# A Mamba scan layer driven by a plan of stages instead of a generator of parts

## The chip, the cores and the metric

The kernel runs on one core of a Trainium2 chip. Its time is device microseconds of one execution, the median of several. The engines that matter here: TensorE (PE, matmuls into PSUM), VectorE (DVE), ScalarE (ACT), GpSimd (POOL), and SyncE (SP), whose queue issues all DMAs of the scan layer.

## The reference, cut to what matters

Four layers run one after the other on x of 3 images, 256 channels, 48 x 48 pixels: an attention block, two 3x3 convolutions, and a Mamba layer. Only the last one is touched by the change. Its input gets a scale and a shift per channel (from the normalisation around each layer), and then, for each image with its 2304 pixels as a sequence of length L:

```python
xn = (xf - mu) * jax.lax.rsqrt(var + 1e-05) * norm_w + norm_b
xz = jnp.einsum('blc,dc->bld', xn, in_proj_w)
x_in, z = jnp.split(xz, 2, axis=-1)
xc = jax.lax.conv_general_dilated(xc, conv_w, ...)   # causal, 4 taps, per channel
u = jax.nn.silu(xc).transpose(0, 2, 1)
x_dbl = jnp.einsum('bld,ed->ble', u, x_proj_w)       # dt_raw (16), B (16), C (16)
dt = jax.nn.softplus(jnp.einsum('blr,dr->bld', dt_raw, dt_proj_w) + dt_proj_b)
def step(hst, inp):
    dA = jnp.exp(dt_t[:, :, None] * A)
    hst = hst * dA + dt_t[:, :, None] * B_t[:, None, :] * u_t[:, :, None]
    y_t = jnp.einsum('bdn,bn->bd', hst, C_t)
y = ys.transpose(1, 0, 2) + u * D_param
y = y * jax.nn.silu(z)
out = jnp.einsum('bld,cd->blc', y, out_proj_w)
```

There are 512 inner channels d with 16 states n each, and the result is added to x.

## The kernel before

All of it is float32. The sequence of each image is cut into 6 chunks of 384 tokens (CH), which makes 18 chunks over the 3 images. A chunk has 16 **steps** j = 4m + g: m is one of 4 blocks of 128 inner channels, g one of 4 groups of states. A step scans 4 x 128 rows of 384 tokens, a row being one channel and one state. The layer has 288 steps.

One step s consists of these instructions:

- `fill(s + 1)` prepares the input dt*B*u of the next step in a tile hs: DVE does one half (L939, reading PSUM tile ps_r, which PE's `spread_pe` L921 has filled), POOL the other (L940).
- DVE runs four scans (L1045), which are called q0 to q3 here. Each needs one decay exp(dt*A), which ACT writes to one of three PSUM banks (`decay`, L952). The decay three scans ahead is issued after each scan.
- ACT keeps the last column of the four scans for the next chunk (L1053). POOL multiplies hs by C into hc (L1056).
- PE adds the four parts of hc of the step before to y in PSUM (`add_states(s - 1)`, L968; at g = 0 a product with D opens the sum, L964).
- In steps with g = 1, DVE multiplies the finished y of the block before by sz, the Silu of z (`gate`, L975), and SP fetches dt and dt*u of the next block, copied over the partitions (`spread`, L912 and L913). The copies come from DRAM, where dt has been written.

Beside the scans of one chunk runs the **preparation** of the next, the generator `prepare`: scale and shift (ACT L770), mean by matmul (PE L778), centring (DVE L780, square on ACT L784), mean of squares (PE L787), inverse root (ACT L789, L790), normalise (DVE L792), tokens (ACT L802), the convolution as four taps times two channel halves of matmuls per block m (PE L823, 16 recorded matmuls per block), taking u to SBUF (ACT L815, L829), z (PE L844, ACT L849), Silu of u and of z back to back (ACT L853, L854), the projection of u (PE L860), B and C through DRAM (ACT L865), dt by matmul in two halves (PE L883), softplus in three ACT passes (L889 to L891), and dt and dt*u (DVE L894, L895, ACT L898). All PSUM results of it use one buffer of two banks, of which `two()` hands out a new tile for each use. Silu lies in another table set of ACT than Exp and Ln, so that a table load stands ahead of the two Silus and another (`exp_ln_tables`, L748) after them. The program calls the generator twice per step, at its very start, ahead of fill and scans, and after hc; each call runs to the next `yield`. Preparation of chunk at + 2 begins in steps 12 to 15 of chunk at.

What is finished of a chunk is projected in steps 2 and 3 of the next one (`project`, PE L988) and both halves stored at step 4, ahead of the fill (`store`, DVE L996); the residual's load is issued at step 1.

Ahead of the first step the whole preparation of chunk 0 and eight parts of chunk 1's (to the tokens) are run through.

`keep_order` ties the instructions of PE, DVE, ACT and POOL to the order in which the program writes them. An instruction whose input isn't there holds up all that is written after it on its engine. The DMAs of SP aren't tied by it.

Of the kernel before, what the change touches and what calls it, by code (L numbers as in the profile page):

```python
# [16 lines left out]
P = 128  # L17
# [60 lines left out]
def net(  # L78
# [618 lines left out]
    with ExitStack() as l3:  # L697
# [52 lines left out]
        def fetch(at):  # L750
            k = chunks[at] = Chunk()
            b, c = todo[at]
            k.xg = act.tile([P, CT, CH], F32, name="xg")
            nc.sync.dma_start(k.xg, xd[b][:, :, c * CH : (c + 1) * CH])
# [4 lines left out]
        def two():  # L759
            return psg.tile([P, 2, 512], F32, tag="g", name="ps_g")  # L760

        def prepare(at, before, k):


            b, c = todo[at]
            sc, sh = norm3[b]
            xg = k.xg

            for ct in range(CT):
                nc.scalar.activation(  # L770
                    xg[:, ct, :], xg[:, ct, :], AF.Identity,
                    bias=sh[:, ct : ct + 1], scale=sc[:, ct : ct + 1],
                )
            yield
            p = two()
            pm, pv = p[:, 0, :CH], p[:, 1, :CH]
            for ct in range(CT):
                nc.tensor.matmul(pm, mean2, xg[:, ct, :], start=ct == 0, stop=ct == CT - 1)  # L778
            yield
            nc.vector.tensor_tensor(  # L780
                xg, xg, pm.unsqueeze(1).broadcast_to([P, CT, CH]), ALU.subtract
            )
            sq = act.tile([P, CT, CH], F32, name="sq", bufs=1)
            nc.scalar.activation(sq, xg, AF.Square)  # L784
            yield
            for ct in range(CT):
                nc.tensor.matmul(pv, mean2, sq[:, ct, :], start=ct == 0, stop=ct == CT - 1)  # L787
            yield
            nc.scalar.activation(pv, pv, AF.Ln, bias=epst)  # L789
            nc.scalar.activation(pv, pv, AF.Exp, scale=-0.5)  # L790
            yield
            nc.vector.tensor_tensor(  # L792
                xg, xg, pv.unsqueeze(1).broadcast_to([P, CT, CH]), ALU.mult
            )
            yield
            xn = k.xn = act.tile([P, CT, CH + DCONV - 1], F32, name="xn")
            if c == 0:
                nc.gpsimd.memset(xn[:, :, : DCONV - 1], 0.0)
            else:
                nc.scalar.copy(xn[:, :, : DCONV - 1], before.xn[:, :, CH:])  # L800
            for ct in range(CT):
                nc.scalar.activation(  # L802
                    xn[:, ct, DCONV - 1 :], xg[:, ct, :], AF.Identity,
                    bias=v("norm_b", ct), scale=v("norm_w", ct),
                )
            yield
            yield
            u = k.u = act.tile([P, DI, CH], F32, name="u")
            for m0 in (0, 2):

                p = None
                for j in range(2):
                    m = m0 + j
                    if j:
                        nc.scalar.activation(  # L815
                            u[:, m0, :], p[:, 0, :CH], AF.Identity, bias=v("conv_b", m0)
                        )
                    yield
                    if not j:
                        p = two()  # L820
                    for tap in range(DCONV):
                        for ct in range(CT):
                            nc.tensor.matmul(  # L823
                                p[:, j, :CH], wtap[:, tap, ct, m * P : (m + 1) * P],
                                xn[:, ct, tap : tap + CH],
                                start=tap == 0 and ct == 0, stop=tap == DCONV - 1 and ct == CT - 1,
                            )
                    yield
                nc.scalar.activation(  # L829
                    u[:, m0 + 1, :], p[:, 1, :CH], AF.Identity, bias=v("conv_b", m0 + 1)  # L830
                )
                if m0 == 0:

                    for _ in range(4):
                        yield

            yield
            sz = k.sz = act.tile([P, DI, CH], F32, name="sz")
            for m0 in (0, 2):
                p = two()  # L840
                for j in range(2):
                    m = m0 + j
                    for ct in range(CT):
                        nc.tensor.matmul(  # L844
                            p[:, j, :CH], w("in", ct * 512 + m * P, P), xn[:, ct, DCONV - 1 :],
                            start=ct == 0, stop=ct == CT - 1,
                        )
                yield
                nc.scalar.copy(sz[:, m0 : m0 + 2, :], p[:, :, :CH])  # L849
                if m0 == 0:  # L850
                    yield

            nc.scalar.activation(u, u, AF.Silu)  # L853
            nc.scalar.activation(sz, sz, AF.Silu)  # L854
            exp_ln_tables()
            yield

            p = two()
            for m in range(DI):
                nc.tensor.matmul(  # L860
                    p[:96, 0, :CH], w("x", m * 96, 96), u[:, m, :], start=m == 0, stop=m == DI - 1
                )
            yield
            dbc = act.tile([96, CH], F32, name="dbc")
            nc.scalar.activation(dbc, p[:96, 0, :CH], AF.Identity, bias=ident[:96, DTR : DTR + 1])  # L865
# [9 lines left out]
            yield  # L875

            dt = act.tile([P, DI, CH], F32, name="dt", bufs=1)
            dtu = k.dtu = act.tile([P, DI, CH], F32, name="dtu")
            for m0 in (0, 2):
                p = two()  # L880
                for j in range(2):
                    m = m0 + j
                    nc.tensor.matmul(  # L883
                        p[:, j, :CH], dtsb[:, m * P : (m + 1) * P], dbc[: DTR + 1, :],
                        start=True, stop=True,
                    )
                yield
                both = dt[:, m0 : m0 + 2, :]
                nc.scalar.activation(both, p[:, :, :CH], AF.Abs)  # L889
                nc.scalar.activation(both, both, AF.Exp, scale=-1.0)  # L890
                nc.scalar.activation(both, both, AF.Ln, bias=1.0)  # L891
                yield
                pdt = p[:, :, :CH]
                nc.vector.scalar_tensor_tensor(pdt, pdt, 0.0, both, ALU.max, ALU.add)  # L894
                nc.vector.tensor_tensor(  # L895
                    dtu[:, m0 : m0 + 2, :], pdt, u[:, m0 : m0 + 2, :], ALU.mult
                )
                nc.scalar.copy(both, pdt)  # L898

            k.dtd = dram.tile([P, DI, CH], F32, name="dtd")  # L900
            nc.sync.dma_start(k.dtd, dt)
            k.dtud = dram.tile([P // 2, DI, CH], F32, name="dtud")
            nc.sync.dma_start(k.dtud, dtu[P // 2 :])
            yield
# [72 lines left out]
        def residual(at):  # L977
            k = chunks[at]
            b, c = todo[at]
            k.ot = act.tile([P, CT, CH], F32, name="ot")  # L980
            nc.sync.dma_start(k.ot, xd[b][:, :, c * CH : (c + 1) * CH])

        def project(at, mo):
            k = chunks[at]
            if mo == 0:
                k.po = two()
            for m in range(DI):
                nc.tensor.matmul(  # L988
                    k.po[:, mo, :CH], w("out", m * 256 + mo * P, P), k.sz[:, m, :],
                    start=m == 0, stop=m == DI - 1,  # L990
                )

        def store(at, mo):
            k = chunks[at]
            b, c = todo[at]
            nc.vector.tensor_tensor(k.ot[:, mo, :], k.po[:, mo, :CH], k.ot[:, mo, :], ALU.add)  # L996
            nc.sync.dma_start(
                out[b, mo * P : (mo + 1) * P, c * CH : (c + 1) * CH], k.ot[:, mo, :]
            )

# [7 lines left out]
        for _ in prepare(0, None, chunks[0]):  # L1008
            pass
        k = chunks[0]  # L1010
        k.rows = {0: spread(k, 0)}
# [4 lines left out]
        parts = {1: prepare(1, k, chunks[1])}  # L1016
        for _ in range(8):
            next(parts[1])

        def part(at):  # L1020
            if at in parts:
                next(parts[at], None)

        for s, (at, m, g) in enumerate(steps):
            k = chunks[at]
            j = 4 * m + g


            if j == 0 and at + 2 <= last:
                fetch(at + 2)  # L1030
            if j == 12 and at + 2 <= last:
                parts[at + 2] = prepare(at + 2, chunks[at + 1], chunks[at + 2])
            mine = at + 2 if j >= 12 else at + 1
            part(mine)
# [151 lines left out]
```

## Time and profile before

| | |
|---|---|
| median of 3 runs | 4667.45 us (4663.21 to 4670.96) |
| the profiled execution | 4670.4 us, span 4668.6 us |
| first fill of the loop over steps | 3001.76 us |
| start of chunk 1 and of chunk 17 | 3093.58 and 4566.38 us |
| end of the last chunk | 4647.95 us |
| DVE scans with a state (L1045) | x960, 998 ns each by the page |
| decays (L952) | x1152, 581 ns |
| hc (L1056) | x288, 3442 ns |
| POOL's half of fill (L940) | x288, 1815 ns |
| DVE's half of fill (L939) | x288, 944 ns |

The page's shares of busy time are averages over four layers: the first 3000 us belong to the attention and the convolutions, in which PE leads. For the scan layer the profile must be read from 3000 us on. Mean durations overlap a little where instructions of one engine follow each other without a gap: a scan takes 1.0 us in the rows, but the next one starts 0.91 us after it. PE's matmuls run at one of two paces: with the granted clock at 1.0 those of 384 columns are some 0.35 us apart, with the clock at 0.5 some 0.64.

### The profile page before, as it was taken

The page shows a single profiled execution, that of the slowest core. Times are in us where ns is not written, and L with a number is a line of the kernel's source. Part 1 is how long each engine was busy: PE and PEld are TensorE (multiplying, and loading weights), DVE is VectorE, ACT ScalarE, POOL GpSimd, SP SyncE. Part 2 cuts the span into 40 slices and gives each one's busy share as a digit, 9 for nine tenths or more (in the row PEclk, how much of TensorE's full clock was granted, in tenths as well). Part 3 has the DMA queues.
Part 4 walks back from the last instruction along what each step waited for, and adds up shares of the span by engine and source line. Part 5 has one row for each costly group of instructions (what it writes and reads, how often), then busy time and mean ns, then how long its engine had stood idle before and what let it go on. Part 6 is the DMA issues. An engine that isn't in the chain of part 4 may idle for free. (4 is left out here: it accounts for less than half of the span.)

```text
span 4668.6 us, 47523 instructions
## 1 busy us (share of the span) xinstructions
PE 3832.0 (82%) x18498; PEld 1603.0 (34%) x18498; DVE 2840.0 (61%) x2936; ACT 2205.5 (47%) x3196; POOL 1547.2 (33%) x662
## 2 busy tenths in 40 slices
PE   7999999789999976269999998677787777778774
PEld 4322222332322222135555554332333233223321
DVE  4677767357686732640001111388888888888887
ACT  1577767137776755200000000366656666665663
POOL 0000000000000001000000000288998899899888
PEclk9999999899999976589999998787888788788875
DMA  2000000000000001310000001233334333343332
GB/s 79 3 1 1 1 1 1 0 1 1 1 1 1 1 28 31 124 61 0 0 0 0 21 20 58 62 92 100 87 94 101 96 90 100 89 104 91 88 94 51
DMA packets 122319, 207.65 MB, mean 44 GB/s; under 512 B 20881, under 2 KB 114129, under 8 KB 118370
## 3 DMA queue, kind: packets, MB, share of 16 engines
q1 hardware_dynamic: 122082, 204.50, 16.2%
q8 instruction: 147, 2.41, 0.2%
q14 instruction: 90, 0.74, 0.1%
HBM read 167.94 MB, written 36.27 MB: 44 GB/s over the span
## 5 line engine op out<-in xcount | busy, mean ns | idle before, releaser
L387 ACT ACTIVATE pt<-ps_s 128x1024 f32<-128x1024 f32 (+1 forms) x1080 | 952.4, 937 | 363.7 <-PE ps_s L383 306.9
L1056 POOL TENSOR_TENSOR hc<-hs,bc 128x1536 f32<-128x1536 f32 x288 | 991.3, 3442 | 170.3 <-DVE hs L1045 154.5
L1045 DVE TENSOR_TENSOR_SCAN hs<-ps_da,hst,hs 128x384 f32<-128x384 f32 x960 | 902.6, 998 | 134.1 <-ACT ps_da L952 131.2
L952 ACT ACTIVATE ps_da<-dtr,amat 128x384 f32<-128x384 f32 x1152 | 653.5, 581 | 363.4 <-DVE hs L1045 345.3
L394 DVE TENSOR_TENSOR part<-part,pt 128x2048 f32<-128x2048 f32 (+1 forms) x360 | 747.8, 2077 | 40.7 <-ACT pt L387 9.4
L147 POOL TENSOR_TENSOR rstd<-ve,mhalf 128x2 f32<-128x2 f32 (+1 forms) x26 | 16.1, 623 | 1957.5 <-DVE ve L145 1957.5
L383 PE MATMUL ps_s<-q,kt 32*128 32x512 f32 (+1 forms) x4320 | 645.2, 603 | 13.0 <-ACT pt L387 7.0
L940 POOL TENSOR_TENSOR hs<-dtur,bc 128x768 f32<-128x768 f32 x288 | 522.6, 1815 | 90.8 <-DMA dtr<-dtd 90.8
L362 PE MATMUL acc<-pt,vt 128*32 128x512 f32 (+1 forms) x4320 | 535.5, 565 | 0.0
L637 PE MATMUL ps_c<-xpad,wmix 128*128 128x384 f32 x1296 | 421.0, 487 | 100.4 <-DVE wmix L678 100.4
L637 PE MATMUL ps_c<-xpad,wconv 128*128 128x384 f32 x1296 | 423.9, 490 | 8.9 <-DVE xpad L623 8.9
L823 PE MATMUL ps_g<-xn,wtap 128*128 128x384 f32 x1152 | 416.1, 516 | 15.1 <-DVE ot L996 5.3
L619 ACT ACTIVATE xpad<-x,gsh,gsc 128x2304 f32<-128x2304 f32 x6 | 13.9, 2320 | 820.7 <-DVE gsh L178 578.2
L968 PE MATMUL ps_y<-hc,rep 128*32 128x384 f32 x2304 | 302.6, 611 | 117.1 <-POOL hc L1056 106.6
L383 PEld LDWEIGHTS ps_s<-q,kt 32*128 32x128 f32 x4320 | 216.4, 184 | 449.4 <-issue 256.2
L637 PEld LDWEIGHTS ps_c<-xpad,wmix 128*128 128x128 f32 x1296 | 246.0, 190 | 274.8 <-DVE wmix L678 100.5
L637 PEld LDWEIGHTS ps_c<-xpad,wconv 128*128 128x128 f32 x1296 | 247.2, 191 | 184.0 <-issue 13.7
L823 PEld LDWEIGHTS ps_g<-xn,wtap 128*128 128x128 f32 x1152 | 224.9, 201 | 219.6 <-issue 26.0
L939 DVE TENSOR_TENSOR hs<-ps_r,bc 128x768 f32<-128x768 f32 x288 | 272.0, 944 | 4.6 <-PE ps_r L921 4.6
L647 DVE TENSOR_TENSOR x<-ps_c,x 128x384 f32<-128x384 f32 x36 | 20.1, 558 | 382.5 <-PE ps_c L637 382.5
L649 DVE SCALAR_TENSOR_TENSOR x<-ps_c,vec,x 128x384 f32<-128x384 f32 x36 | 22.2, 618 | 370.5 <-PE ps_c L637 370.5
L613 POOL MEMSET xpad<- 128x100 f32 x12 | 2.6, 216 | 674.7 <-PE ps_c L637 526.8
(180 smaller groups left out, 3543.1 us busy)
## 6 DMA issues: line engine op xcount, KB each, us to landing
dtr<-dtd SPq DMA_DIRECT2D x288, 192.0 KB, 3.8
bc<-bcd SPq DMA_DIRECT2D x144, 192.0 KB, 4.9
dtur<-dtud SPq DMA_DIRECT2D x288, 96.0 KB, 3.0
wconv<-in_we SPq DMA_DIRECT2D x16, 1152.0 KB, 7.4
dtd<-dt SPq DMA_DIRECT2D x18, 768.0 KB, 3.5
xb<-in_x SPq DMA_DIRECT2D x6, 1152.0 KB, 12.0
xc<-in_x SPq DMA_DIRECT2D x18, 384.0 KB, 3.2
xd<-x SPq DMA_DIRECT2D x3, 2304.0 KB, 8.3
```

The costliest lines, as they stand in the source:

```text
L362: nc.tensor.matmul(acc[r, :n], vt[:, mt, g * P + h * HD : g * P + (h + 1) * HD], p[:, h, :n], start=first, stop=last,)
L383: nc.tensor.matmul(s[:, j, :n], kt[r, mt * P : (mt + 1) * P], q[r, :n], start=True, stop=True,)
L387: nc.scalar.activation(p[:, h0 : h0 + 2, :n], s[:, :, :n], AF.Exp)
L394: nc.vector.tensor_tensor(part[:, :, :n], part[:, :, :n], p[:, :, :n], ALU.add)
L637: nc.tensor.matmul(pc[:, :CH].rearrange("p (r c) -> p r c", c=HW), wt[:, ct, tap * 256 + m * P : tap * 256 + (m + 1) * P], xp[:, ct, c * R ...
L823: nc.tensor.matmul(p[:, j, :CH], wtap[:, tap, ct, m * P : (m + 1) * P], xn[:, ct, tap : tap + CH], start=tap == 0 and ct == 0, stop=tap == ...
L939: nc.vector.tensor_tensor(hs[:, 0:2, :], k.ps[:, :, :CH], bb, ALU.mult)
L940: nc.gpsimd.tensor_tensor(hs[:, 2:4, :], k.rows[m][1], bb, ALU.mult)
L952: nc.scalar.activation(da[:, :CH], chunks[at].rows[m][0][:, q, :], AF.Exp, scale=amat[:, col : col + 1])
L968: nc.tensor.matmul(k.y_ps[32 * q : 32 * q + 32, :CH], fold, hc[:, q, :], start=False, stop=g == 3,)
L1045: nc.vector.tensor_tensor_scan(hs[:, q, :], decays[q][:, :CH], hs[:, q, :], 0.0 if todo[at][1] == 0 else state[m, g][:, q : q + 1], ALU.mu ...
L1056: nc.gpsimd.tensor_tensor(hc, hs, cb, ALU.mult)
```

## The change

The generator is replaced by a table `plan` of stages. Each line names a step j, a place in it, the chunk that is prepared (2: the one after the next, 1: the next) and the stage. There are three places: MID, between the second and the third scan of the step (after the decay that follows the second scan), LATE, after hc, and PE_, after `add_states`. A second table `after` does the same for the work on finished chunks. Stages that read what PE has produced stand in MID; matmuls stand in PE_.

With it come these changes:

- One tile `bank` of two PSUM banks stands for the whole layer in place of the tiles of `two()`. Stages use bank 0 or 1 of it by turns (block m uses bank m % 2).
- Convolution of the four blocks: one block per step, in steps 1 to 5; u is taken in the steps 3, 4, 5 and 6.
- Silu of u at step 7 of the chunk before, Silu of sz only at step 2 of its own chunk, each with its own pair of table loads.
- z is projected in steps 12 to 14, after dt, and no longer ahead of Silu.
- Projection of a finished chunk at steps 6 and 7, stores at 7 and 8 one by one; residual's load at step 4; the load of a new chunk's x at step 2.
- `add_states(s - 2)` instead of s - 1, three buffers of hc instead of two, the gate after the second scan in steps with g = 2.
- Ahead of the first step chunk 1 gets only the first stages, to the mean of squares.

The core of the diff:

```diff
-            p = two()
-            pm, pv = p[:, 0, :CH], p[:, 1, :CH]
+        bank = psg.tile([P, 2, 512], F32, name="ps_g")
...
+        plan = [
+            (13, MID, 2, group_scale),
+            (14, PE_, 2, lambda k: channel_mean(k.xg, 0)),
+            (15, MID, 2, centre),
+            (15, PE_, 2, lambda k: channel_mean(k.sq, 1)),
+            (0, MID, 1, inverse_root),
+            (0, LATE, 1, normalise),
+            (1, MID, 1, tokens),
+            (1, PE_, 1, lambda k: taps(k, 0, 0, 2)),
+            (2, PE_, 1, lambda k: taps(k, 0, 2, 4)),
+            (3, MID, 1, lambda k: take_u(k, 0)),
+            (3, PE_, 1, lambda k: taps(k, 1, 0, 4)),
+            (4, MID, 1, lambda k: take_u(k, 1)),
+            (4, PE_, 1, lambda k: taps(k, 2, 0, 4)),
+            (5, MID, 1, lambda k: take_u(k, 2)),
+            (5, PE_, 1, lambda k: taps(k, 3, 0, 4)),
+            (6, MID, 1, lambda k: take_u(k, 3)),
+            (7, MID, 1, lambda k: silu(k.u)),
+            (7, PE_, 1, project_u),
+            (8, MID, 1, take_dbc),
+            (8, PE_, 1, lambda k: project_dt(k, 0)),
+            (9, MID, 1, lambda k: softplus(k, 0)),
+            (9, LATE, 1, lambda k: take_dt(k, 0)),
+            (10, PE_, 1, lambda k: project_dt(k, 2)),
+            (11, MID, 1, lambda k: softplus(k, 2)),
+            (11, LATE, 1, lambda k: take_dt(k, 2)),
+            (12, PE_, 1, lambda k: project_z(k, 0)),
+            (13, MID, 1, lambda k: take_z(k, 0)),
+            (13, PE_, 1, lambda k: project_z(k, 2)),
+            (14, MID, 1, lambda k: take_z(k, 2)),
+        ]
+        after = [
+            (2, MID, 0, lambda k: silu(k.sz)),
+            (4, MID, -1, residual),
+            (6, PE_, -1, lambda k: project_y(k, 0)),
+            (7, MID, -1, lambda k: store(k, 0)),
+            (7, PE_, -1, lambda k: project_y(k, 1)),
+            (8, MID, -1, lambda k: store(k, 1)),
+        ]
...
+        def silu(t):
+            nc.scalar.activation(t, t, AF.Silu)
             exp_ln_tables()
...
-        for _ in range(8):
-            next(parts[1])
+        for _, _, rel, stage in plan:
+            if rel == 2:
+                stage(chunks[1])
...
                 decay(4 * s + q + 3)
+                if q == 1:
+                    if g == 2 and s >= 6:
+                        gate(*steps[s - 6][:2])
+                    run(at, j, MID)
...
-            hc = tiles[s] = scn.tile([P, 4, CH], F32, name="hc")
+            hc = tiles[s] = scn.tile([P, 4, CH], F32, name="hc", bufs=3)
             nc.gpsimd.tensor_tensor(hc, hs, cb, ALU.mult)
-            part(mine)
...
-            if s:
-                add_states(s - 1)
+            run(at, j, LATE)
+            if s >= 2:
+                add_states(s - 2)
+            run(at, j, PE_)
```

265 lines of the change are left out of this document (112 added, 153 removed).

## The prediction

> **What bounds the kernel now.** I read first the windows of the scan layer, in 200 us stretches from its first step (3002 us) on. Columns: stretch, length, busy time with count of PE, weight loads, DVE, ACT and POOL, then the clock.
>
> ```profile
> 3400.00:3600.00 200.00, 153.22 (x603) 64.54 (x601) 174.62 (x201) 124.48 (x216) 181.78 (x73) 0.85 0.38 95
> 3600.00:3800.00 200.00, 151.69 (x578) 62.67 (x578) 172.24 (x198) 129.28 (x236) 178.40 (x71) 0.82 0.39 96
> ```
>
> DVE is busy 87%, POOL 90%, neither all the time: the layer runs at DVE's own work plus the waits that end on DVE. So I took one chunk, 3640.72 to 3732.9 us, and asked for its waits (engine, line, waited for: us, times, longest):
>
> ```profile
> ACT ps_da L952 <- DVE hs L1045: 18.0, 37, 3.8
> DVE hs L1045 <- ACT ps_da L952: 10.0, 5, 4.7
> POOL hc L1056 <- DVE hs L1045: 9.6, 5, 3.8
> DVE ot L996 <- PE ps_g L988: 1.7, 1, 1.7
> ```
>
> POOL waits for DVE, not DVE for POOL: POOL's two instructions start 5.17 us apart in all (1.81 + 3.44, overlapping slightly), 82.7 us for 16 steps. DVE's five waits for a decay are ACT held up by something else. Which, the timeline of DVE and ACT in that chunk tells (start, duration, in brackets the idle time before it):
>
> ```profile
> 3659.78 1.01 DVE L1045 TENSOR_TENSOR_SCAN hs<-ps_da,hst,hs 128x384 f32<-128x384 f32 x1 [1.07 <-ACT ps_da L952]
> 3667.30 1.02 DVE L996 TENSOR_TENSOR ot<-ps_g,ot 128x384 f32<-128x384 f32 x2 [1.72 <-PE ps_g L988]
> 3689.58 1.28 ACT L853 ACT_TABLE_LOAD   x1
> 3690.88 1.48 ACT L853 ACTIVATE u<-u 128x1536 f32<-128x1536 f32 x1
> 3692.27 1.47 ACT L854 ACTIVATE sz<-sz 128x1536 f32<-128x1536 f32 x1
> 3693.75 1.28 ACT L748 ACT_TABLE_LOAD   x1
> 3695.66 1.02 DVE L1045 TENSOR_TENSOR_SCAN hs<-ps_da,hst,hs 128x384 f32<-128x384 f32 x1 [4.71 <-ACT ps_da L952]
> 3714.96 1.02 DVE L1045 TENSOR_TENSOR_SCAN hs<-ps_da,hst,hs 128x384 f32<-128x384 f32 x1 [3.36 <-ACT ps_da L952]
> ```
>
> The pair of Silus costs DVE 4.71 us, the second softplus 3.36, a take of u 1.07, the first store 1.72; three small ones (0.47, 0.39, 0.18) make 11.9. From starts in the same timeline DVE's own pitches are 0.86 for a fill and 0.91 for a scan (0.85 in the first chunk of an image), so 4.50 a step (4.26 there), 72.0 for 16; gates 4 x 0.45, stores 0.9, centre 0.87, normalise 0.85, two takes of dt 3.72: 80.15 together. 80.15 + 11.9 = 92.05, and chunks 1 to 16 take just that (starts 3093.58 and 4566.38: 1472.8 / 16). Chunk 0 takes 91.8 (3001.76 to 3093.58).
>
> **The change part by part.** DVE's own work stays 80.15; what counts is the list of waits, worked out anew along one chunk, time 0 being the start of its step 2.
>
> Silu of sz at step 2: ACT reaches it at 3.41 (fill 0.86, two scans 1.82, decay 0.58, gaps) and holds load, Silu, load, 4.06 with gaps, until 7.5. The next decay ends at 8.1, the scan wanted it at 6.72: a wait of 1.40.
>
> Taps. The wait list of the changed program shows each take of u ahead of the next taps, although they use different banks, because both are one tile. One channel block then costs a round of taps and take; the prologue, which runs that way already, shows the pitch:
>
> ```profile
> 2928.62 0.58 ACT L815 ACTIVATE u<-ps_g,vec 128x384 f32<-128x384 f32 x1 [6.82 <-PE ps_g L823]
> 2929.25 5.43 PE L823 MATMUL ps_g<-xn,wtap 128*128 128x384 f32 x16 [0.67 <-ACT u L815]
> 2934.72 0.58 ACT L829 ACTIVATE u<-ps_g,vec 128x384 f32<-128x384 f32 x1 [5.52 <-PE ps_g L823]
> 2947.55 2.85 PE L844 MATMUL ps_g<-xn,w3sb 128*128 128x384 f32 x8 [0.67 <-ACT u L829]
> 2954.17 0.80 ACT L849 COPY sz<-ps_g 128x768 f32<-128x768 f32 x1 [2.94 <-PE ps_g L844]
> ```
>
> 6.10 us, and 6.14 with the fold of a step in between (0.78, beside the take). The plan gives each block one step, 4.50. Before, the two pairs of blocks lie four steps apart. The first take can start at 9.8 (ACT free at 9.7; the taps before it end at 7.6 plus 1.0 to 2.7 for a cold clock, estimated from a group of 16 that took 7.01 at 3645.50 instead of 5.43). Three rounds: 28.2 for the last take. PE then has spread 0.84, diagonal 0.74, fold 0.78 and the first half of project_y 2.78: the first store gets its sum at 33.3. DVE, delayed by the 1.40 alone, would be there at 27.5: a wait of 5.8, spread over steps 4 to 7. Silu of u at step 7 falls in this time (ACT 31.0 to 35.1, DVE's next decay not needed before 35.6) and costs nothing; were the cover gone, it would cost the 1.40 of the other Silu.
>
> Second store: project_y's second half waits for the first store, 2.78; project_u behind it on PE, 2.6, is waited for as well (same tile): 39.4 against DVE at 38.25, 1.17.
>
> Softplus: ACT in mid step, DVE at the end of the same step. Decay 0.63 and three passes of 0.84 and gaps, 3.3 in all, against two scans of 1.82: 1.48, twice. Behind the DVE instruction wait the next fill and with it POOL. The second pair of matmuls comes after an idle PE: 2.9 cold instead of 1.57 with part of it hidden, +0.91. The z projection, now at steps 12 to 14, runs cold before the mean; the centre at step 15 waits 0.1 to 1.5, I take 1.0, nearer the cold rows of that stretch.
>
> Sum: 1.40 + 5.8 + 1.17 + 2.96 + 0.91 + 1.0 = 13.2 of waits against 11.9; 93.3 us per chunk. With all terms at their lower ends 92.35, at the upper ends (cold taps 0.5, cold PE before the second softplus and centre 0.8) 94.6.
>
> Fold two steps behind, three hc buffers and the gate in mid step cost nothing: PE has the fold's input one step earlier than it needs it, which covers POOL's 3.44. Without that cover DVE wouldn't wait either until a gate, 0.45 on DVE, is late. The residual's load moved from step 1 to 4 has three steps (13 us) before the store; fetch has eleven steps. On SP only the last half of a spread stands behind the first store; it is wanted 15 us later.
>
> Prologue: z and its copies stood on the path, 2947.55 to 2954.97, 7.4 us. Now they lie beside the dt round trip through memory (ACT idle 11.63 us before the first decay at 2989.69), and a cold clock there may return 1. Of chunk 1 only the steps to the mean of squares remain ahead: the next fill can follow the centre (2994.94 + 0.87) and not normalise (fill at 3001.76), 5.95. Together 13.35 at most, 12.4 at least; I take 13.1. Silu of sz gains nothing: it lay under project_u.
>
> Chunk 0 has no stores and no gate of a chunk before it (-1.35) and the faster scans (-3.84): 74.95 of work. Its waits: Silu of sz 1.9, taps 3.75, Silu of u 1.9 (no store covers it), the rest 5.0: 87.5 against 91.8, -4.3. The two other first chunks save about 2.3 each against 93.3, outside the chain of taps: -4.6. The last chunk's first store waits for a cold project_y, 3.9 against 3.4 and a little: +0.7.
>
> Total: -13.1 - 4.3 - 4.6 + 0.7 + 16 x (93.3 - 92.05 = 1.25) = -1.3. The profiled execution took 4670.4 (span 4668.6 and 1.8 around it), 2.95 above the median 4667.45. So 4669.1 by its own time, **4666** against the median.
>
> [...]
>
> **Rivals.** (1) Slower: the cold clock falls into the chain of taps. Place: steps 1 to 8; price: one group of 16 that runs at half pace, up to 5.3 us (5.27 doubled), enters the first store's wait whole. It decides from 94.0 per chunk on. For it: matmuls of the chunk at 3640 run at double pitch in about a quarter of it (project_u 4.51 at 3692.41 against 2.6 warm); half-microsecond windows show the clock at half from 3600.9 to 3604.3 and full until 3611.2, steps of 3.41 us; chunks settle at 92.16, 27 of these, in the second half of the layer, so a chunk may be drawn to 28, 95.57: 16 x 3.5 - 17 = +39, 4707. Against: PE is nearly without gaps from step 1 to 8.
>
> (2) Faster by a lock the other way: chunks again settle at 92.16, the first chunks of images too: -13.1 - 4.3 + 0.7 + 1.8 = -15, 4652. For it: table loads before are 460.8 us apart over five chunks. Against: the list's lower end, 92.35.
>
> (3) Faster by cover: waits that I add singly hide each other, as where POOL's lag already delays DVE; both softplus waits and the centre's gone, 4.9 per chunk, gives 4588; half of it 4627. Against: before, such waits add up to 11.9 with nothing left over.
>
> (4) The banks do overlap, that is the waits of one bank don't hold the other. Then 0.3 in the taps and 1.17 at the second store go, 4643. The wait list speaks against it; I give it 0.02, within (3).
>
> **How the numbers follow.** A measurement of this kernel can tell about 0.2%, 9.3 us. My list of waits: 0.48, over 92.35 to 94.6, 4651 to 4687; from 92.8 to 94.0 the time is within 0.2%, so faster 0.12, same 0.24, slower 0.12. Rival 1 0.27; rival 2 0.16; rival 3 with 4 0.09. Faster 0.37, same 0.24, slower 0.39. The range takes in 28 windows with 4 us on it, 4710, and half of rival 3 with a little less, 4632; what is outside is the rest of rival 3 and a worse rival 1.
>
> **What would show it.** Right: a chunk of 93.3; the largest wait on DVE before the first store (3 us) with ACT's takes of u 6.1 apart; two waits of 1.5 before the takes of dt; four table loads per chunk, one pair costing DVE 1.4; first step near 2989. Wrong: takes of u more than 6.5 apart, taps cold (rival 1); DVE waits under 10 us a chunk (rival 3); project_u running before the first store ends would refute the waits of the tile. The total is wrong if a chunk is off by more than 0.6 us.

## The result and the profile after

The changed kernel takes 4701.22 us (median of 4 runs, 4691.87 to 4703.47), the kernel before beside it 4669.2: the ratio is 1.0067, with an interval of 1.0049 to 1.0084. It is slower by 32 us, where I forecast no change; the time lies within the range.

The profiled execution is the fastest of the four, 4691.87 us. Its first three layers ended early: the first centring of the scan layer starts at 2904.30 us, before at 2912.28. So I count from there to the start of the last two stores: 1749.8 us before, 1779.1 after, 29.3 more.

The windows of the scan layer that were shown of before, now of the changed kernel (busy PE, weight loads, DVE, ACT, POOL, then the clock):

```profile
3400.00:3600.00 200.00, 151.98 (x592) 63.77 (x590) 170.09 (x196) 127.29 (x215) 173.15 (x68) 0.83 0.37 94
3600.00:3800.00 200.00, 148.43 (x549) 62.24 (x550) 168.86 (x194) 126.26 (x229) 174.30 (x68) 0.79 0.40 97
```

DVE and POOL do the same work in a longer time: both are less busy than before (174.62 and 181.78 in the first of these windows). Nothing new became a bound; waits grew. One chunk, from one second store (3881.72) to the next (3977.29), 95.57 us, by its waits (us, times, longest):

```profile
POOL hc L1079 <- DVE hs L1064: 12.5, 5, 4.2
DVE hs L995 <- PE ps_r L977: 5.4, 3, 2.6
DVE ps_g L869 <- ACT dt L865: 3.6, 2, 2.3
DVE hs L1064 <- ACT ps_da L1008: 2.2, 2, 1.5
DVE ot L907 <- PE ps_g L829: 2.1, 2, 1.1
DVE ot L907 <- PE ps_g L896: 1.6, 1, 1.6
DVE xg L781 <- PE ps_g L775: 0.3, 1, 0.3
```

The second store's row counts the store at either end of the window, so one 1.07 belongs to the chunk. In all DVE waits 14.2 us here; the chunk of before that ends at 3944.14, counted the same way, waits 11.2 of 92.2. Of DVE's rows the one of L995 is new: its half of the fill waits for the spread of PE (ps_r, L977), three times, 5.4 us; before, this was 0.2. One of the three, 2.60, stands behind the taps and belongs to what I had forecast there; 2.29 in step 14 and 0.49 in step 2 do not. (I name such a fill by the step of its spread; it opens the step after.)

Where the 2.29 comes from, the timeline of steps 12 to 14 shows (start, duration, in brackets the idle time before it and its releaser), and below it the clock in three windows of the same time (third column from the end, 1.00 or 0.5):

```profile
3906.55 4.54 PE L884 MATMUL ps_g<-xn,w3sb 128*128 128x384 f32 x8 [2.81 <-ACT dt L873]
3913.35 1.29 ACT L768 ACTIVATE xg<-xg,norm 128x384 f32<-128x384 f32 x2
3914.55 0.77 ACT L892 COPY sz<-ps_g 128x768 f32<-128x768 f32 x1
3915.38 5.49 PE L884 MATMUL ps_g<-xn,w3sb 128*128 128x384 f32 x8 [3.51 <-ACT sz L892]
3920.80 1.02 PE L977 MATMUL ps_r<-dtu,rep 32*128 32x384 f32 x4
3921.87 0.96 DVE L995 TENSOR_TENSOR hs<-ps_r,bc 128x768 f32<-128x768 f32 x1 [2.29 <-PE ps_r L977]
```

```profile
3911.00:3913.00 2.00, 0.87 (x9) 0.16 (x8) 2.00 (x3) 0.75 (x2) 2.00 (x1) 1.00 0.48 131
3914.00:3920.00 6.00, 4.62 (x7) 2.52 (x8) 5.58 (x7) 3.59 (x8) 6.00 (x3) 0.52 0.52 119
3921.00:3930.00 9.00, 7.05 (x38) 2.32 (x38) 7.83 (x9) 5.54 (x11) 6.91 (x3) 1.00 0.47 117
```

PE stands idle for 3.51 us: the take of z's first half stands in the middle of step 13, and ACT scales the next chunk's x (1.29) ahead of it. Meanwhile the clock falls to half (1.00 in the first of the three windows, 0.52 in the second). Z's second half then takes 5.49 instead of 2.85, the spread for the next chunk is behind it in PE's order, and DVE waits 2.29 for the spread. So it goes in 12 of the chunks 1 to 16; averaged over all 16 the fill behind z waits 1.86.

The waits that I had worked out are there as well. The dense stretch (take of u and first store) and the Silu of sz:

```profile
3966.76 0.96 DVE L995 TENSOR_TENSOR hs<-ps_r,bc 128x768 f32<-128x768 f32 x1 [2.60 <-PE ps_r L977]
3971.15 0.56 DVE L907 TENSOR_TENSOR ot<-ps_g,ot 128x384 f32<-128x384 f32 x1 [1.60 <-PE ps_g L896]
3974.51 2.74 PE L829 MATMUL ps_g<-u,w3sb 128*96 128x384 f32 x8
3977.29 0.56 DVE L907 TENSOR_TENSOR ot<-ps_g,ot 128x384 f32<-128x384 f32 x1 [1.07 <-PE ps_g L829]
3940.93 1.28 ACT L823 ACT_TABLE_LOAD   x1
3942.23 1.48 ACT L823 ACTIVATE sz<-sz 128x1536 f32<-128x1536 f32 x1
3945.64 2.83 DVE L1064 TENSOR_TENSOR_SCAN hs<-ps_da,hst,hs 128x384 f32<-128x384 f32 x3 [0.69 <-ACT ps_da L1008]
```

| stretch of the scan layer | forecast | before | after | change |
|---|---|---|---|---|
| first centring to the first fill of the loop | -13.1 | 89.48 | 77.64 | -11.8 |
| chunk 0 | -4.3 | 91.82 | 90.64 | -1.2 |
| chunks 1 to 16, mean of one | +0.96 | 92.05 | 94.82 | +2.77 (44.3 in all) |
| chunk 17 and the end | +0.7 | 95.70 | 93.64 | -2.1 |
| sum | -1.3 | 1749.8 | 1779.1 | +29.3 |

(The forecast for a mean chunk is 1.25 less the 4.6 of the two first chunks of images, spread over 16.)

### The profile page after: what moved, and what is told of

It is laid out like the page before. It is cut to its first block, busy times and chain, and to the rows that moved or that the text cites. A ratio compares the mean times of both kernels' runs of the same rounds, so it can differ in the third digit from the quotient of the medians.

```text
span 4690.1 us, 47677 instructions
## 1 busy us (share of the span) xinstructions
PE 3855.1 (82%) x18498; PEld 1615.9 (34%) x18498; DVE 2844.3 (61%) x2936; ACT 2241.5 (48%) x3232; POOL 1548.3 (33%) x662
## 5 line engine op out<-in xcount | busy, mean ns | idle before, releaser
L811 PE MATMUL ps_g<-xn,wtap 128*128 128x384 f32 x1152 | 432.0, 529 | 83.1 <-ACT xn L802 70.1
L1024 PE MATMUL ps_y<-hc,rep 128*32 128x384 f32 x2304 | 291.3, 591 | 65.5 <-POOL hc L1079 63.4
L995 DVE TENSOR_TENSOR hs<-ps_r,bc 128x768 f32<-128x768 f32 x288 | 270.3, 939 | 96.1 <-PE ps_r L977 96.0
L884 PE MATMUL ps_g<-xn,w3sb 128*128 128x384 f32 x288 | 170.7, 764 | 110.2 <-ACT sz L892 55.5
```

What stands on the lines that cost most here:

```text
L811: nc.tensor.matmul(bank[:, m % 2, :CH], wtap[:, tap, ct, m * P : (m + 1) * P], k.xn[:, ct, tap : tap + CH], start=tap == 0 and ct == 0, st ...
L995: nc.vector.tensor_tensor(hs[:, 0:2, :], k.ps[:, :, :CH], bb, ALU.mult)
L1024: nc.tensor.matmul(k.y_ps[32 * q : 32 * q + 32, :CH], fold, hc[:, q, :], start=False, stop=g == 3,)
```

## The experiments

Each ratio is against runs of the kernel before on the same chip. A difference to the changed kernel is one of medians; the kernel before measured 4665 to 4669 us beside them, so up to 4 us of such a difference says nothing.

**Do waits and work add up, or is a chunk a whole number of clock steps?** Two kernels add DVE work to the kernel before, once and twice, at one step of each chunk:

```diff
-            nc.vector.tensor_tensor(hs[:, 0:2, :], k.ps[:, :, :CH], bb, ALU.mult)
+            for _ in range(2 if 4 * m + g == 13 else 1):   # 3 in before_fill2
+                nc.vector.tensor_tensor(hs[:, 0:2, :], k.ps[:, :, :CH], bb, ALU.mult)
```

> The kernel before with DVE's half of the fill of step 13 done twice, 0.86 more of DVE per chunk, nothing else changed. Theory A, waits and work add up: 17 x 0.86 = 14.6, 4684. Theory B, a chunk is 27 steps of 3.41 us whatever it holds within limits: less than 3 more, 4669 to 4672, the waits in the chunk shorter by 0.86 together.

> The same with that fill done three times, 1.72 more of DVE per chunk. Theory A: 29 more, 4698. Theory B: either nothing (27 steps of 3.41 still hold it) or a whole step, 16 x 3.4 = 55 more, 4724; not 29.

Measured: 4682.25 us, 1.0035 (1.0021 to 1.0049), and 4702.32, 1.0080 (1.0064 to 1.0095): 15 and 34 us more for 14.6 and 29 us of added work. From the first centring to the end it is 14.3 and 32.6 more. A chunk is not held at 27 steps of the clock: added work comes out. But that the first total fits so well is partly luck. Chunks 1 to 16 took 19.7 and 37.0 more for 13.8 and 27.5 of added work, and the stretches ahead of and behind them came out shorter by 5.4 and 4.5 with nothing taken from them. So the list of waits is a usable sum to about 0.6 us a chunk, some 10 us in the kernel; finer differences it can't price.

**Z one step earlier.**

```diff
-            (12, PE_, 1, lambda k: project_z(k, 0)),      # and the three lines after it
+            (11, PE_, 1, lambda k: project_z(k, 0)),
```

> The changed kernel with the four z stages one step earlier (steps 11 to 13). Theory A, waits in PE's order: z at half clock stands ahead of the next chunk's spread, DVE's fill behind it waits 2.29 in step 14 (and 0.49 in step 2); with a step more for z the 2.29 goes, a chunk takes 93.3 instead of 95.57 and the kernel about 4665. Theory B, a chunk settles at a whole number of the clock's steps of 3.41 us (28 now): it goes to 27, 92.16, and the kernel to about 4647, or stays at 28 and 4701 with another wait grown by what this one loses. Rival C, the two passes of Silu or the dense taps cost the time: stays near 4701 with the fill's wait gone and no other grown.

Measured: 4685.24, 1.0046 (1.0031 to 1.0061), 16 less than the changed kernel. The fill's 2.29 is gone, but the one at step 2 has 1.07 instead of 0.49, and the second softplus still waits 2.29; the listed chunk takes 93.9. A scan's wait is new: in step 12 ACT's take of z stands ahead of the decays and waits for z's first half, which runs slow (4.46 a chunk earlier, at 3900.48, with the clock at 0.50 until 3903.8; the second half, behind it, 2.85):

```profile
3999.72 0.80 ACT L892 COPY sz<-ps_g 128x768 f32<-128x768 f32 x1 [2.94 <-PE ps_g L884]
4001.04 2.83 DVE L1064 TENSOR_TENSOR_SCAN hs<-ps_da,hst,hs 128x384 f32<-128x384 f32 x3 [1.29 <-ACT ps_da L1008]
```

Over chunks 1 to 16 it averages 0.98, half of the 1.86 that the fill had. Theory A holds in direction and for its own wait; its 36 us don't, for the most part since z's first half now makes another instruction wait.

**Z's first half taken ahead of the scale**, the exchange of two ACT instructions in step 13:

```diff
-            for when, where, rel, stage in after + plan:
+            for when, where, rel, stage in after + sorted(plan, key=lambda p: p[2]):
```

> The changed kernel with one pair of ACT stages exchanged: in step 13 z's first half is taken ahead of the scale of the next chunk's x (1.29 on ACT), not behind it. If z's second half is late because of its start (after ACT's take) and its half clock, it starts 1.2 earlier: the fill's wait of 2.29 goes to about 1.0 and a chunk to 94.3, 4680. If the clock's edges set its end (it runs until the clock is full again), the wait stays at 2.3 and the time at 4701.

Measured: 4665.20, ratio 1.0000 (0.9991 to 1.0009): 36 us less than the changed kernel by two instructions in another order. The timeline of this kernel, same place:

```profile
3895.52 0.79 ACT L892 COPY sz<-ps_g 128x768 f32<-128x768 f32 x1
3896.21 1.30 ACT L768 ACTIVATE xg<-xg,norm 128x384 f32<-128x384 f32 x2
3896.37 2.85 PE L884 MATMUL ps_g<-xn,w3sb 128*128 128x384 f32 x8 [1.02 <-ACT sz L892]
3899.15 0.91 PE L977 MATMUL ps_r<-dtu,rep 32*128 32x384 f32 x4
```

PE is idle 1.02 and not 3.51, z's second half runs at full clock (2.85; the clock reads 1.00 from 3894.9 on), and no fill waits behind it in any of the chunks 1 to 16. In this chunk the second softplus waits 1.31 instead of 2.29, since dt's second half met the full clock too (1.55 instead of 2.92); in 9 of the 16 chunks the wait is 2.3 as before. The fill at step 2 waits 1.11. I had expected half of the effect: the earlier start, not the clock.

**Idle matmuls against the half clock.**

```diff
+            if 4 * m + g in range(6, 16):
+                for _ in range(6):
+                    nc.tensor.matmul(
+                        k.y_ps[:, CH:], diag[:, m, :], k.u[:, m, :P], start=False, stop=False)
             for q in range(4):      # the folds
```

> The changed kernel with six idle matmuls in each of the steps 8 to 15, 0 and 1 (into unused columns of the y bank, read by nobody), ahead of the folds, so that PE isn't idle long enough for its clock to be halved. Theory A, the half clock makes z late: the clock reads 1.0 from step 10 on, z takes 2.85 instead of 5.5, the fill's waits (2.29 and 0.49) and 1.0 of the second softplus go: 91.8 a chunk, about 4640. Theory B: the tie to steps of 3.41 us goes with the half clock, chunks of first pieces of an image get shorter by their 3.8 us of faster scans again. Rival C, PE has too much work: takes of u and the stores wait longer, slower than 4701.

Measured: 4729.65, 1.0136 (1.0119 to 1.0152), 28 slower than the changed kernel. Two lines of its timeline tell why:

```profile
3926.66 1.68 PE L855 MATMUL ps_g<-dbc,dtsb 17*128 17x384 f32 x4
3930.97 0.97 DVE L869 SCALAR_TENSOR_TENSOR ps_g<-ps_g,dt 128x768 f32<-128x768 f32 x1 [3.61 <-ACT dt L865]
```

Dt's second half takes 1.68 instead of 2.92, the first half of z 2.85 instead of 4.54, and the fill behind z waits 1.19 instead of 2.29: the half clock does make these late (the mean granted clock of the profiled execution is 0.916, in the changed kernel 0.881). (Z's second half, after 3.87 us of idle PE, still takes 4.24.) But the idle matmuls stand in PE's order too. Dt starts 18.9 us after the second store instead of 16.4, and the softplus waits 3.61, the centring 1.65. Rival C's sign, by another place than it named.

**Project_u behind the second store.**

```diff
-            (7, PE_, 1, project_u),
-            (8, MID, 1, take_dbc),              # project_dt(k, 0) 8 to 9,
+            (8, PE_, 1, project_u),             # softplus and take_dt(k, 0) 9 to 10
+            (9, MID, 1, take_dbc),
```

> The changed kernel with project_u, the take of B and C, the first half of dt and its softplus each one step later (into the step that was free), so that no matmul of project_u stands between project_y's second half and the second store. If the second store waits because project_u writes the same tile, its wait of 1.07 goes to 0 and the chunk from 95.57 to 94.5, about 4683. If it waits for project_y itself, the wait stays and the time too. The price may be a later second half of dt: its softplus wait, 2.3 now, up to 0.6 longer, then 4692.

Measured: 4654.75, 0.9968 (0.9957 to 0.9979), 46 less than the changed kernel and below the kernel before. The second store waits for nothing now; a line of the timeline, to be set beside the changed kernel's at 3977.29 with its 1.07:

```profile
3959.70 0.54 DVE L907 TENSOR_TENSOR ot<-ps_g,ot 128x384 f32<-128x384 f32 x1
```

So the wait was for project_u, which uses the other bank of the same tile. That explains 1.07 a chunk, 18 us. The rest lies in other waits, whose cause was not tested apart: fills behind the spread 1.23 instead of 2.29 and 0.49 (z's second half 4.54 instead of 5.49), softplus 0.85 and 1.98 instead of 1.31 and 2.29; the Silu of sz waits 0.6 more.

**The fold one step behind**, with what belongs to it:

```diff
-            if s >= 2:
-                add_states(s - 2)
+            if s >= 1:
+                add_states(s - 1)
...
-                    if g == 2 and s >= 6:
-                        gate(*steps[s - 6][:2])
+                    if g == 1 and s >= 5:
+                        gate(*steps[s - 5][:2])
```

(and hc with two buffers)

> The changed kernel with the fold one step behind again, two hc buffers and the gate in steps with g = 1. If this part costs and brings nothing (my reading), the time stays within 5 us of 4701 and the list of waits as it is. If the fold two steps behind is what keeps PE from waiting for POOL, folds of step s-1 wait for hc in PE's order and the taps behind them come later: waits at the taps and the first store grow by up to 3.4 (one hc) in the dense steps 3 to 6, up to 4750.

Measured: 4643.19, 0.9952 (0.9936 to 0.9967), 58 less than the changed kernel. Both theories are wrong: the part that I costed at nothing is the dearest. PE in step 10 of the changed kernel, and then of this one:

```profile
3894.49 0.53 DVE L1031 TENSOR_TENSOR sz<-ps_y,sz 128x384 f32<-128x384 f32 x1
3895.07 1.65 PE L1020 MATMUL ps_y<-u,diag 128*128 128x384 f32 x2 [0.54 <-DVE sz L1031]
3896.65 1.51 PE L1024 MATMUL ps_y<-hc,rep 128*32 128x384 f32 x8
3898.09 2.92 PE L855 MATMUL ps_g<-dbc,dtsb 17*128 17x384 f32 x4
```

```profile
3867.55 1.65 PE L977 MATMUL ps_r<-dtu,rep 32*128 32x384 f32 x4 [2.42 <-DVE hs L995]
3869.13 1.51 PE L1024 MATMUL ps_y<-hc,rep 128*32 128x384 f32 x8
3870.57 2.92 PE L855 MATMUL ps_g<-dbc,dtsb 17*128 17x384 f32 x4
```

With the fold two steps behind, a block's first fold comes in the step with g = 2, and the product with D (L1020) that opens the sum must wait for the gate in the middle of that step. Dt's second half stands behind it. One step behind, the product falls in steps with g = 1; in step 9 nothing urgent follows it, and dt starts 14.1 us after the second store instead of 16.4. The 0.54 of idle PE and the product's own 1.58 (3895.07 to 3896.65) make 2.1 of these 2.3; dt's second half takes 2.92 in both. In the listed chunk of 91.66 the waits are 10.55:

```profile
3938.45 0.96 DVE L995 TENSOR_TENSOR hs<-ps_r,bc 128x768 f32<-128x768 f32 x1 [3.72 <-PE ps_r L977]
3942.00 0.56 DVE L907 TENSOR_TENSOR ot<-ps_g,ot 128x384 f32<-128x384 f32 x1 [0.76 <-PE ps_g L896]
3946.58 1.02 DVE L1064 TENSOR_TENSOR_SCAN hs<-ps_da,hst,hs 128x384 f32<-128x384 f32 x1 [0.42 <-ACT ps_da L1008]
3948.14 0.56 DVE L907 TENSOR_TENSOR ot<-ps_g,ot 128x384 f32<-128x384 f32 x1 [0.54 <-PE ps_g L829]
```

The rest is softplus 0.85 and 1.31, step 2 1.88, a take of u 1.07. No fill waits behind z in any chunk; z's second half takes 2.85 in the listed one (3888.69, the clock at 1.00). Averaged over chunks 1 to 16 the changes are: fill behind z 1.86 to 0, both softplus waits 3.61 to 2.19, both stores 2.72 to 1.33; against this the fill in step 6 grows from 2.63 to 3.74, the one in step 2 from 0.60 to 1.28.

**The gate alone, one scan earlier**, to tell the product with D from the age of hc:

```diff
-                if q == 1:
-                    if g == 2 and s >= 6:
-                        gate(*steps[s - 6][:2])
+                if q == 0 and g == 2 and s >= 6:
+                    gate(*steps[s - 6][:2])
+                if q == 1:
```

> The changed kernel with the gate one scan earlier in its step (after the first scan, not the second). Theory G: the fold two steps behind costs because the product with D, which opens the next sum, then waits in steps with g = 2 for the gate in mid step, and dt's second half (step 10) and project_y (step 6) stand behind it on PE. Then the second half of dt starts 0.9 earlier (15.5 after the second store instead of 16.4), the second softplus waits 1.3 to 1.4 instead of 2.3, and z starts earlier too: 94 or less a chunk, 4685 or less. Theory H: it is the age of hc alone (PE's order, POOL), then 0.9 of the gate changes nothing, 4701.

Measured: 4681.97, 1.0030 (1.0019 to 1.0041), 19 less. The second softplus waits 1.69 instead of 2.29, the fill behind z 1.19 instead of 2.29; a new wait of 1.01 is the gate's own for the last fold. Dt's second half starts 15.8 us after the second store. The moment of the gate matters, so theory G is right in its direction. It accounts for 19 of the 58; what is left of them, the product with D out of these steps altogether, the gate on DVE in the step of the first softplus, or the fold's own age, was not taken apart further.

**Do the gains add up?** The fold one step behind together with z taken first, with project_u later, and with both:

> The fold one step behind and z taken ahead of the scale. Each alone frees the fill behind z (2.3) and 1.0 of the second softplus. If both work through the same thing, z and dt at half clock, the two together bring no more than the better one: 4643 within 6. If their gains add up, 4607.

> The fold one step behind and project_u one step later. By the list of waits the second store's 0.54, and with it 0.42 of Silu of u, goes: 0.5 to 1 a chunk, 4627 to 4635. If the gains of the two added up, 4597; if project_u one step later brings the half clock to dt, as in the kernel with that edit alone (second softplus 1.98), 4643 or more.

> All three edits. Work of 81.1 and waits: softplus 0.85 and 1.3, step 2 1.9, taps and first store 1.1, 3.7 and 0.8: 9.6, a chunk of 90.7, 4630. If waits return elsewhere as in the evenly spread plan, a chunk of 91.4, 4643.

Measured: 4639.26, 0.9943 (0.9928 to 0.9959); 4655.77, 0.9974 (0.9965 to 0.9983); 4652.08, 0.9969 (0.9959 to 0.9979). Alone they win 58, 36 and 46; together with the fold z wins 62, project_u 45, and all three 49. The gains don't add up, because they win mostly the same waits: the fill behind z, 1.86 a chunk on average, is 0 with the fold alone, 0 with z alone and 1.02 with project_u alone, and both softplus waits together, 3.61, are 2.19, 3.21 and 2.76. For z this is the clock (its second half takes 2.85 in the listed chunks with the fold and with z taken first); for dt it is not, since with the fold dt's second half still takes 2.92 in the listed chunk (3870.57, the clock at 0.50) and only starts earlier. With the fold, project_u later takes some 10 us back (0.9974 against 0.9952): the gate is in step 9 and no longer fills the first softplus' wait, which moved to step 10 (1.31, not 0.85), and dt's second half follows its first after one step instead of two (second softplus 1.98, not 1.31). All three together miss both figures of their expectation, 4630 and 4643. The same three edits without the fold:

> The changed kernel with the three edits together: project_u and the first half of dt a step later, z a step earlier, z taken ahead of the scale. By the waits of the kernel with the first edit (11.15 in a chunk of 92.26) the 1.23 of the fill behind z goes: 91.0, 20 us less than that kernel's 4655, 4635. If z taken earlier runs into the second softplus or shifts the half clock into the taps, as its 0.6 at step 2 in the kernel with z earlier alone suggests, 91.6, 4645.

Measured: 4663.74, 0.9997 (0.9988 to 1.0006). The fill's 1.23 in step 14 went, a fill in step 2 got 1.05, and takes 0.86 and 0.32: more than the kernel with project_u alone, which neither 4635 nor 4645 had allowed for.

**The dense stretch thinned out.** Three plans that spread the taps, described in their expectations; here the core of the second, with the fold two steps behind:

```diff
+            (2, PE_, 1, lambda k: taps(k, 1, 0, 2)),
+            (3, PE_, 1, lambda k: taps(k, 1, 2, 4)),
+            (4, PE_, 1, lambda k: taps(k, 2, 0, 4)),
+            (5, PE_, -1, lambda k: project_y(k, 0)),
+            (6, PE_, 1, lambda k: taps(k, 3, 0, 4)),
             (7, PE_, -1, lambda k: project_y(k, 1)),
```

> The changed kernel with another plan from chunk 2 on: preparation one step earlier, taps of the first two blocks in halves over four steps, z's first half in step 9 beside the free step of dt, its second half in step 12, the second take of dt in mid step 12, Silu of sz in step 3. If the changed kernel's time is its list of waits, these shrink: taps and first store 5.75 to about 3.7, the fills behind z 2.8 to 0.5, the second softplus 2.3 to 0, second store 1.07 and first softplus 1.3 stay, Silu of u may appear with up to 1.4: 14.2 to 8 or 9.5, a chunk of 90 to 91, 4610 to 4630, below both kernels. If something else sets the pace (POOL, or ACT with its four table loads), the waits return elsewhere and the time stays above 4660.

> The changed kernel with PE's work spread evenly, from chunk 2 on: preparation one step earlier, taps of blocks 0 and 1 in halves over steps 0 to 3, block 2 in step 4, project_y's first half in step 5, block 3 in step 6, second half in 7, project_u 8, dt 9 and 10, z 11 and 12. If the chunk is work plus list of waits: taps and stores 5.5 to about 1, Silu of u uncovered 1.3, Silu of sz 1.3, softplus 0.85 and 2.0, centre and fills 0.5: 7 and 81.3, 88 a chunk, about 4590. If POOL (82.7 us of work a chunk) with its lag already sets the pace, the chunk stays at 90 or more and DVE waits for POOL's half of the fill, 4620 or more.

> The changed kernel with the fold one step behind and, from chunk 2 on, preparation one step earlier: block 0 in steps 0 and 1, blocks 1 and 2 in steps 2 and 3, block 3 in halves in steps 4 and 5, z in steps 11 and 12, Silu of sz in step 1. If PE's dense stretch sets the waits there, the spread of step 6 is no longer behind a whole block: 3.7, 0.8 and 0.9 of the kernel with the fold alone go to about 2, Silu of u may show 1.3, softplus 0.85 and 1.3, step 2 at most 1.5: 7 to 8, 89 a chunk, 4600. If waits return elsewhere, as in the evenly spread plan, 91 a chunk and 4640.

Measured: 4655.87, 0.9975 (0.9965 to 0.9985); 4661.24, 0.9988 (0.9979 to 0.9997); 4644.29, 0.9952 (0.9938 to 0.9965). None comes near its 4590 to 4630; the third ends at the other figure of its expectation, 91 a chunk and 4640. In the first, z's first half in step 9 stands ahead of the spread of step 10, and a fill waits 2.61. In the second the waits at taps and first store fall from 5.75 to 0.76, and the Silu of u, no longer covered, shows whole:

```profile
3955.38 1.28 ACT L823 ACT_TABLE_LOAD   x1
3956.67 1.48 ACT L823 ACTIVATE u<-u 128x1536 f32<-128x1536 f32 x1
3958.18 1.28 ACT L748 ACT_TABLE_LOAD   x1
3960.09 1.02 DVE L1101 TENSOR_TENSOR_SCAN hs<-ps_da,hst,hs 128x384 f32<-128x384 f32 x1 [4.48 <-ACT ps_da L1045]
```

I had priced the lost cover at 1.3; together with the take of u just ahead of it on ACT it is 4.48. In the third the waits are more and smaller (2.10, 1.72, 1.31, 1.29, 1.28 and less), 9.7 together.

**Silu of sz alone in its own pass**, in the kernel before:

```diff
-            nc.scalar.activation(sz, sz, AF.Silu)
...
                 decay(4 * s + q + 3)
+                if j == 2 and q == 1:
+                    nc.scalar.activation(k.sz, k.sz, AF.Silu)
+                    exp_ln_tables()
```

> The kernel before with only the Silu of sz moved to step 2 of its own chunk, with a pair of table loads of its own. By the rows of both kernels: the wait of 4.71 loses the 1.47 of the second Silu, 3.24, and a wait of 0.7 (the changed kernel's) to 1.4 appears at step 2: 0.1 to 0.8 a chunk less, 17 chunks 2 to 13 us, 4655 to 4665. Rival, the split costs more than the Silu that it moves, because two more loads of 1.28 stand on ACT: 1.1 to 2.6 more a chunk, 4686 to 4711.

Measured: 4660.55, 0.9981 (0.9972 to 0.9990), 8 us faster. The wait of 4.71 becomes 3.34, and the new pass costs 2.12 at step 2, 1.72 of which the first store's wait gives back. The two extra loads are 1.28 long each; the Silu of sz starts 0.02 us behind the first (3933.04), the next decay 0.02 behind the second (3935.84).

**The long prologue back**, in the changed kernel:

```diff
-        for _, _, _, stage in plan:
+        for _, _, _, stage in plan[:16] + plan[-4:] + plan[16:-4]:
             stage(k)
...
-        for _, _, rel, stage in plan:
-            if rel == 2:
-                stage(chunks[1])
+        for _, _, _, stage in plan[:7]:       # and not again in chunk 0
+            stage(chunks[1])
```

> The changed kernel with the long way to the first step restored: z of chunk 0 ahead of Silu, and inverse root, normalise and tokens of chunk 1 ahead of the first step. If what the shorter prologue gains reaches the end, the first fill is back near 3002 (2988 now) and the kernel 13 us slower than the changed one, 4714, less up to 2 for the first chunk's relieved DVE. If chunks take it up in their waits, 4701.

Measured: 4704.24, 1.0078 (1.0063 to 1.0094), 3 us slower than the changed kernel. The first fill is 9.4 later (87.03 after the first centring instead of 77.64), but chunks 0 to 2 are 3.3, 1.9 and 1.1 shorter. Of 9.4 us won ahead of the loop some 3.4 are left at the end of the profiled execution; the medians can't tell so little from nothing.

## Why the prediction was wrong

- **Taps, first store, second store, Silu of u: right.** 5.8 was forecast, 1.54 + 2.61 + 1.60 = 5.75 is there; 1.17 forecast, 1.07 there, and project_u later took it away. Silu of u costs nothing while covered.
- **Silu of sz, softplus, centre: right in kind, too dear.** 0.69 for 1.40 (the fill's 0.49 just ahead of it makes DVE late and hides as much); 1.31 and 2.29 for 1.48 and 2.39; 0.31 for 1.0.
- **"Fold two steps behind, three hc buffers and the gate in mid step cost nothing": the step that failed.** I looked at who waits for the fold, not at what stands behind it. Undoing the three together wins 58 us. I named DVE's gate as the only thing that could be late; but the product with D waits for the gate, and dt and project_y stand behind it on PE. By the run with the gate one scan earlier this wait is worth 19 us; which part of the three the other 39 belong to stays open.
- **Z at steps 12 to 14: the missing term.** I saw that z runs at half clock and charged the centre 1.0 for it. The spread of step 14 is behind z as well, and ahead of a fill: 2.29, and 0.49 at step 2 (on average 1.86 and 0.60), which were not in the list. This is the row that the sum lacked, and an exchange of two ACT instructions removes 36 us, more than the whole slowdown. It is not a second 36 beside the 58: the fold one step behind frees the same fill, and the two together win 62.
- **Rival 1: right about the clock, wrong about its place, and about the lock.** Its price, 4707, is near, and with it the range took in 4701; that is luck. The taps of steps 3 to 5 ran at full clock (5.43 for each group, from 3948.16, 3954.30 and 3960.44, with the clock at 1.00 from 3941.53 to 3982.49); the half clock fell on dt (second half 2.92) and z (second half 5.49). And that a chunk is drawn to 28 clock steps is refuted in that form: the kernels with added fills leave 27, and the chunks of the changed kernel take from 93.4 to 95.8. The chunks of before vary too, from 90.8 to 93.1, around the 92.16 that I read as 27 steps.
- **Prologue: -13.1 forecast, -11.8 there at the first fill.** As a part of the sum it was too large: by the profile of the run with the long prologue two thirds of such a gain are lost again in chunks 0 to 2.
- **First chunks of the images: too cheap.** 87.5 was forecast for chunk 0 and 91.0 for the two others; they take 90.6 and 94.1. The waits listed above, softplus 1.45 and 2.66 and the taps with a fill of 2.79 among them, stand in chunk 0 too, 14.5 in all where I had 12.6; its other time is 1.2 longer, which I did not trace.
- In the sum: waits of a listed chunk 14.2, not 13.2; before, counted the same way, 11.2, not 11.9; and DVE's time outside waits 0.3 more. That makes 3.4 a chunk instead of 1.3.

## What to carry to other kernels

When a step is moved on an in-order engine, list what stands behind it there, and price the wait of those, not only of its own readers: here a product of 0.8 us behind a gate was part of 58 us. Where PE's matmuls come one group per step, ask which of them start after several microseconds of idle PE, and keep what is urgent from standing behind them: z's second half took 5.49 us behind 3.51 us of idle PE and 2.85 behind 1.02; the order of two small ACT instructions was worth 36 us. The best kernel found is the changed one with the fold one step behind and z taken first, 4639 us, 0.9943 of before; 4643 with the fold alone can't be told from it.

## What the runs showed of the hardware

I had weighed a tie of single chunks to the clock's steps (rivals 1 and 2); what these runs show is a tie of whole images. In most of these kernels the chunk times repeat from image to image, and then an image, from the start of chunk 6 to that of chunk 12, takes a whole number of steps of 3.413 us to within 0.05: 552.92 us before (162 steps are 552.96), 570.03 after (167: 570.03), 563.20 with z earlier (165: 563.20), 556.37 with z taken first (163: 556.37). The added fills moved it to 559.8 and 566.6, 164 and 166 steps. Where the pattern doesn't repeat, as with the fold one step behind (547.5 to 547.8, 160.4 to 160.5 steps), there is no such number. The step is the clock's: in the scan layer of the traces before and after the clock reads 1.00 or 0.50, in 107 and 130 stretches, and each of these lasts a whole number of steps of 3.413 us to within 0.001. From the middle of the chunk read above on it turns at 3903.99, 3907.40, 3910.81, 3914.22, 3921.05, 3931.29, 3941.53 and 3982.49, 23 steps in 78.50 us. That the loop falls into step through its waits behind matmuls of either pace is my reading; no run isolates it. Changes of its work come through, but not to scale: 5.2 and 10.3 us of added fills lengthened an image by 2 and 4 steps, 6.9 and 13.7 us. A step per image is 10 us in the kernel.
